# Relative-position products of both head groups in one 64-column matmul, columns before rows

## The chip, the cores and the metric

The kernel runs on one core of a Trainium2 chip. A core has TensorE (PE in the profile, with its weight loads listed apart as PEld), VectorE (DVE), ScalarE (ACT), GpSimd (POOL) and SyncE (SP), which here issues nearly all DMA transfers. Each engine works through its own list in order, and semaphores hold an instruction back until what it needs is there. The metric is the time of one execution on the device in microseconds (us), as the median of several runs. Lower is better.

## The reference

Eight images of 32x32 positions and 256 channels pass a first layer (group norm; a 3x3 convolution to 192 channels; beside it an attention of 8 heads with relative positions, 64 channels), then a second layer (layer norm, single-head attention over the 1024 positions), then a mixture of experts. What matters here is the relative part of the first attention. For every head and every query position, the logits get a term by the column distance and a term by the row distance:

```
rel = jnp.einsum('bnxyd,md->bnxym', q, rel_k)      # 63 distances m, 8 numbers d per head
rel = rel_to_abs(rel)                              # distance -> absolute column (or row) of the key
...
logits = jnp.einsum('bnid,bnjd->bnij', qf, kf)
logits = logits + rel_w + rel_h
weights = jax.nn.softmax(logits, axis=-1)
```

## The kernel before

**Stages.** For each image b the first part runs `first_layer(b)` and then `second_layer(b)`; after all eight images come the experts. The order on each engine is written out by hand. `fill.send(us)` puts pieces of the convolution (`pc`, line 481) or of the values (`pvv`, line 451) of an image between other work, by a fixed budget of microseconds and not by what is idle, so TensorE's list does not adapt to how long things take.

**Units.** The attention of the first layer is done in four `Unit`s per image: two halves of the queries by two groups g of four heads (HG = 4, NG = 2). A Unit's operand `F` is loaded by DMA when the Unit is made: lines 503 from the DRAM tile `fds` (keys' queries and the column features) and lines 507 from the DRAM tile `fys` (the row features). It is 2 x 768 KB and 4 x 128 KB. `score` (line 522) multiplies F with `KM` and DVE takes the maximum (line 529).

**The relative products.** `features(b, qs, qx)` makes what goes into `fds` and `fys`. It is a generator that is advanced eight times per image (a *piece* each). `qs` holds the queries of both groups row by row; `qx` is the same turned column by column, which GpSimd copies from `qs` (line 400). For each group and for each of rows (`which == 0`, table `bhs`, named `th` in the trace) and columns (`which == 1`, `bws`, `tw`), there are 32 matmuls, one for each row or column i, with a slice of the table as the stationary operand and 32 queries as the moving one (line 419). They fill one PSUM tile `prel` of 2 x 512 columns. A piece is 16 of these matmuls. After 32, the tile leaves PSUM in two halves: ACT copies each to `rel` rounded to fp32r (line 436), DVE writes the remainder beside it (line 437), and SP sends `rel` to `fys` (line 440) or `fds` (line 444).

**Where the pieces stand.** Pieces 1 and 2 of the next image stand at the end of `first_layer`. Pieces 3 to 8 stand in the first six of the eight steps of `second_layer`, called it0 to it5 here. A step (`Attention.scores`) is: the logits `lg` (line 754, four matmul passes of 512 columns), their maximum (757) and its scaling (758) on DVE, the exponential `pr` on ACT (760), then `beside()`, which advances the generator and sends some convolution, and then `turn()`, which transposes the exponentials of the step before (772) and copies them to `pt` (775 on DVE, 777 on ACT). Every second step, `finish` forms the product of a block of 256 queries with the values (`po`, line 832), ACT copies it to `os` (836), and TensorE multiplies it with the output weights (`pa`, 843). Unit 0 of the next image is made after piece 4, Unit 1 after piece 8; their first scores stand in the steps it6 and it7.

**Buffers that tie these together.** `lg_tile` hands out two PSUM tiles of two banks, in turn, to `lg`, `prel` and many others. A `prel` tile is held from its first piece until DVE has read it. `pt_tile` hands out three SBUF tiles for the `rel` tiles and for the `pt` of the blocks. Before, the `rel` of piece 6 takes the buffer that the first block's `pt` leaves, so its copy waits for that block's `po`.

At the start (image 0) there is nothing beside the pieces but convolution: `fill.send(1.5)` and `next(rel)` four times, then Unit 0, four times, then Unit 1.

Of the kernel before, what the change touches and what calls it, by code (L numbers as in the profile page):

```python
# [10 lines left out]
FP = mybir.dt.float32  # L11
FR = mybir.dt.float32r
I32 = mybir.dt.int32
AF = mybir.ActivationFunctionType
ALU = mybir.AluOpType
# [3 lines left out]
P = 128  # L19
B, HH, WW, C = 8, 32, 32, 256  # L20
S = HH * WW
# [3 lines left out]
HG = 4  # L25
NG = NH // HG
# [12 lines left out]
def kernel(  # L39
# [26 lines left out]
    nc = tc.nc  # L66
# [40 lines left out]
    with ExitStack() as ph:  # L107
        wp = ph.enter_context(tc.tile_pool(name="wp", bufs=1))
        work = ph.enter_context(tc.tile_pool(name="work", bufs=1))
# [16 lines left out]
        def lg_tile(name):  # L126
            return ps_lg.tile([P, 2, 512], FP, tag="lg", name=name)
# [7 lines left out]
        def pt_tile(name, dt=FP):  # L135
            return work.tile([P, 2048], dt, tag="pt", name=name, bufs=3)
# [69 lines left out]
        rel = []  # L206
        M = 2 * HH - 1
        for n, table in (("h", key_rel_h), ("w", key_rel_w)):
# [7 lines left out]
            tab = pt_tile(f"tab{n}")  # L216
# [11 lines left out]
            t = wp.tile([P, M * HG], FR, tag=f"t{n}", name=f"t{n}")  # L228
# [4 lines left out]
        bhs, bws = rel  # L233
# [177 lines left out]
        def features(b, qs, qx):  # L411


            for g in range(NG):
                for which in range(2):
                    pr = lg_tile("prel").rearrange("p a s -> p (a s)")
                    tab, src = ((bhs, qs), (bws, qx))[which]
                    for i in range(32):
                        nc.tensor.matmul(  # L419
                            pr[:, i * 32 : (i + 1) * 32],  # L420
                            lhsT=tab[:, (WW - 1 - i) * HG : (2 * WW - 1 - i) * HG],
                            rhs=src[:, g, i * 32 : (i + 1) * 32],
                            start=True,
                            stop=True,
                        )
                        if i == 15:
                            yield None
                    t = pt_tile("rel", FR).rearrange("p (l s) -> p l s", l=2)
                    for half in range(2):
                        c = slice(half * 512, (half + 1) * 512)  # L430
                        if which == 0:
                            ps, hi, lo = pr[:, c], t[:, 0, c], t[:, 1, c]
                        else:
                            ps = pr.rearrange("p (x y) -> p y x", y=HH)[:, half * 16 : half * 16 + 16, :]
                            hi, lo = (t[:, l, c].rearrange("p (y x) -> p y x", x=WW) for l in range(2))
                        nc.scalar.copy(hi, ps)  # L436
                        nc.vector.tensor_tensor(lo, ps, hi, ALU.subtract)  # L437
                    tb = t.bitcast(FP)
                    if which == 0:
                        nc.sync.dma_start(out=fys[b % 2][g].rearrange("l p s -> p l s"), in_=tb)  # L440
                    else:
                        dst = fds[b % 2][g][R_M * HG : (R_M + 64) * HG].rearrange("(l p) s -> p l s", p=P)
                        for p in (slice(HG, 64), slice(64, P)):
                            nc.sync.dma_start(out=dst[p], in_=tb[p])
                    yield None

        def values(b):
            pv = mi_tile("pvv").rearrange("p (j c) -> p j c", c=DK)
# [354 lines left out]
        def second_layer(b, sec, rel):  # L803
            more = b + 1 < B
            st2 = work.tile([P, NT, 6], FP, tag="lst2", name="lst2")
            units = []
            if more:
                fill.dense.insert(min(1, len(fill.dense)), values(b + 1))
            pieces = [2]

            def beside():
                if more and pieces[0] < 8:
                    next(rel)
                    pieces[0] += 1
                    if pieces[0] in (4, 8):
                        units.append(Unit(b + 1, pieces[0] // 4 - 1))
                    fill.send(0.6)
                else:
                    ahead(2)

            def ahead(n):
                for _ in range(n if units else 0):
                    units[0].score()
                fill.send(0.6)

            att.beside = beside
            for ib in range(S // IB):

                def finish(pt, rc, ib=ib):
                    po = ps_po.tile([P, 512], FP, tag="po", name="po1")  # L830
                    for jc in range(NT):
                        nc.tensor.matmul(  # L832
                            po[:, 0:IB], lhsT=sec.v[:, jc, :], rhs=pt[:, jc, :], start=jc == 0, stop=jc == NT - 1
                        )
                    os = work.tile([P, 512], FP, tag="os", name="os1")[:, 0:IB]
                    nc.scalar.copy(os, po[:, 0:IB])
                    if ib >= 2:
                        ahead(2)
                    else:
                        fill.send(0.8)  # L840
                    pa = st_tile("pa1").rearrange("p (i c) -> p i c", c=C)
                    for i in range(NIB):
                        nc.tensor.matmul(
                            pa[:, i, :], lhsT=os[:, i * P : (i + 1) * P], rhs=wo, start=True, stop=True
                        )
                    for i in range(NIB):
                        tt = T[b][:, ib * NIB + i, :]
                        nc.vector.scalar_tensor_tensor(tt, pa[:, i, :], rc[:, i : i + 1], tt, ALU.mult, ALU.add)
                        nc.vector.bn_stats(st2[:, ib * NIB + i, :], tt)

                blk = Block(finish)
                for i in range(NIB):
                    it = ib * NIB + i
                    att.scores(blk, i, sec.qk[:, 0, it * P : (it + 1) * P], sec.qk[:, 1], blk.rs, 1.0 / math.sqrt(U))
            ahead(2)
            att.drain(ahead)
            sums[b] = st2
            return units
# [36 lines left out]
        with tc.manual_schedule():  # L895
            nc.scalar.preload_act_table_set(LNEXP)
            fill.chains.append(normalise(0))
            while fill.chains:
                fill.send(1.0)
            rel = features(0, *queries(0))  # L900
            keys(0)
            fill.dense.insert(min(1, len(fill.dense)), values(0))
            units = []
            for g in range(NG):
                for i in range(4):
                    fill.send(1.5)
                    next(rel)
                units.append(Unit(0, g))
            fill.send(5.0)
            for b in range(B):  # L910
                sec, rel = first_layer(b, units)
                units = second_layer(b, sec, rel)
            fill.chains.append(token_mean(B - 1))
            fill.finish()
# [273 lines left out]
```

## Time and profile before

| | |
|---|---|
| median of 3 runs | 2906.44 us (2900.96 to 2912.57) |
| the profiled execution: time, and span from its first to its last instruction | 2906.21 us, 2904.4 us |
| busy share of the span: PE, PEld, DVE, ACT, POOL | 88%, 58%, 45%, 33%, 10% |
| matmuls of line 419, and mean granted TensorE clock | 1024; 0.96 of full speed |

Busy shares are sums over an engine's list; matmuls are pipelined and their ends modelled, so a busy PE is not a PE at its peak. Which work sets the end is read from the chain that ended last, and, at one place, from the timeline: each line there has the start, the duration, the engine, the source line, the operation, the tiles, and in square brackets the idle time before it and who ended that.

### The profile page before, as it was taken

The page shows a single profiled execution, that of the slowest core. Times are in us where ns is not written, and L with a number is a line of the kernel's source. Part 1 is how long each engine was busy: PE and PEld are TensorE (multiplying, and loading weights), DVE is VectorE, ACT ScalarE, POOL GpSimd, SP SyncE. Part 2 cuts the span into 40 slices and gives each one's busy share as a digit, 9 for nine tenths or more (in the row PEclk, how much of TensorE's full clock was granted, in tenths as well). Part 3 has the DMA queues.
Part 4 walks back from the last instruction along what each step waited for, and adds up shares of the span by engine and source line. Part 5 has one row for each costly group of instructions (what it writes and reads, how often), then busy time and mean ns, then how long its engine had stood idle before and what let it go on. Part 6 is the DMA issues. An engine that isn't in the chain of part 4 may idle for free.

```text
span 2904.4 us, 30948 instructions
## 1 busy us (share of the span) xinstructions
PE 2560.5 (88%) x12395; PEld 1685.4 (58%) x12395; DVE 1296.2 (45%) x2327; ACT 965.3 (33%) x1679; POOL 301.0 (10%) x196
## 2 busy tenths in 40 slices
PE   4899879997998799979987998799889769999998
PEld 3865665565656555655475556555654346666665
DVE  4454256426643564366335634662457252333232
ACT  0045214531452145214521552154225422223222
POOL 3011001100110011001100110011000021111110
PEclk7899889999999999999999999999999989999999
DMA  3621233133313321342144114312421031112110
GB/s 99 140 56 38 65 80 74 29 70 94 71 31 80 90 56 31 87 97 42 30 90 99 38 36 95 88 38 41 108 55 30 1 106 58 58 58 73 58 51 22
DMA packets 89761, 186.12 MB, mean 64 GB/s; under 512 B 8161, under 2 KB 36714, under 8 KB 87314
## 3 DMA queue, kind: packets, MB, share of 16 engines
q1 hardware_dynamic: 86962, 182.04, 26.6%
q8 instruction: 98, 1.61, 0.2%
q10 hardware_dynamic: 2656, 2.10, 0.2%
q14 instruction: 45, 0.37, 0.0%
HBM read 112.15 MB, written 62.52 MB: 60 GB/s over the span
## 4 chain that ended last, share of the span: by engine, by line
PE 76%; DVE 15%; ACT 5%; DMA 2%; issue 2%; SPq 1%; POOL 0%; ACTq 0%; DVEq 0%
PE pc L481 11%; PE po L573 9%; PE st L558 9%; PE py L1115 8%; PE phd L1097 8%; DVE mx L529 6%; PE lg L522 6%; PE prel L419 4%; PE po L832 4%; PE lg L754 3%; PE pq L653 2%; ACT PT L565 2%; PE tp L772 2%; PE pmean L874 1%; DMA T<-in_x_dram 1%
## 5 line engine op out<-in xcount | busy, mean ns | idle before, releaser
L565 ACT ACTIVATE PT<-st 128x512 f32<-128x512 f32 x1024 | 598.5, 598 | 492.5 <-PE st L558 452.9
L529 DVE TENSOR_REDUCE mx<-lg 128x1 f32<-128x1024 f32 x512 | 603.7, 1217 | 296.0 <-PE lg L522 295.9
L481 PE MATMUL pc<-convw,gpad 128*128 128x192 f32 x2304 | 506.0, 341 | 55.1 <-DVE T L489 33.6
L558 PE MATMUL st<-F,KM 128*128 128x512 f32 x1024 | 479.7, 474 | 19.6 <-ACT PT L565 11.6
L481 PEld LDWEIGHTS pc<-convw,gpad 128*128 128x128 f32 x2304 | 404.3, 196 | 109.5 <-DVE T L489 42.7
L522 PE MATMUL lg<-KM,F 128*128 128x512 f32 x1024 | 345.5, 424 | 73.9 <-ACT pr L760 32.9
L558 PEld LDWEIGHTS st<-F,KM 128*128 128x128 f32 x1024 | 192.2, 190 | 297.3 <-ACT PT L565 177.4
L573 PE MATMUL po<-PT,vk 128*32 128x512 f32 x2048 | 284.0, 617 | 0.0
L522 PEld LDWEIGHTS lg<-KM,F 128*128 128x128 f32 x1024 | 184.4, 190 | 143.0 <-DVE mx L529 50.3
L1115 PE MATMUL py<-w,hT 128*128 128x256 f32 x1024 | 237.3, 385 | 0.0
L1097 PE MATMUL phd<-n2T,w 128*128 128x512 f32 x512 | 222.9, 593 | 0.0
L1115 PEld LDWEIGHTS py<-w,hT 128*128 128x128 f32 x1024 | 189.9, 190 | 45.6 <-issue 22.4
L1122 DVE TENSOR_TENSOR r<-py,n 128x256 f32<-128x256 f32 x64 | 27.2, 425 | 308.4 <-PE py L1115 308.4
L1097 PEld LDWEIGHTS phd<-n2T,w 128*128 128x128 f32 x512 | 97.0, 191 | 115.5 <-issue 108.4
L352 POOL TENSOR_TENSOR T<-T,l0b 128x2048 f32<-128x2048 f32 x8 | 36.5, 4558 | 1145.2 <-PE tpx L311 1145.2
L591 DVE RECIPROCAL rc<-pa 128x16 f32<-128x16 f32 x32 | 8.3, 258 | 307.1 <-PE pa L588 307.1
L760 ACT ACTIVATE pr<-lg,nm 128x1024 f32<-128x1024 f32 x64 | 71.4, 1115 | 201.8 <-DVE nm L758 201.8
L754 PE MATMUL lg<-nqk 128*128 128x512 f32 x256 | 129.8, 633 | 0.0
L437 DVE TENSOR_TENSOR rel<-prel,rel 128x512 fp32r<-128x512 f32 x64 | 44.3, 692 | 190.6 <-ACT rel L436 190.6
L641 POOL TENSOR_TENSOR T<-T,n 128x256 f32<-128x256 f32 x64 | 48.3, 774 | 755.1 <-DVE n L638 755.1
L832 PE MATMUL po<-pt,v 128*128 128x256 f32 x512 | 121.1, 391 | 0.4 <-DVE pt L775 0.4
L1104 ACT ACTIVATE hT<-phd,b1c 128x512 f32<-128x512 f32 x128 | 86.3, 686 | 97.6 <-PE phd L1097 97.4
(223 smaller groups left out, 2441.4 us busy)
## 6 DMA issues: line engine op xcount, KB each, us to landing
F<-fd SPq DMA_DIRECT2D x64, 768.0 KB
fy<-rel SPq DMA_DIRECT2D x16, 1024.0 KB
F<-fy SPq DMA_DIRECT2D x128, 128.0 KB
w<-in_L_ffn_W_dram SPq DMA_DIRECT2D x32, 512.0 KB
T<-in_x_dram SPq DMA_DIRECT2D x8, 1024.0 KB
scr<-kqh SPq DMA_DIRECT2D x64, 128.0 KB
fd<-kqh SPq DMA_DIRECT2D x32, 256.0 KB
KM<-kd SPq DMA_DIRECT2D x32, 256.0 KB
```

Of the source, the lines that this page charges most:

```text
L419: nc.tensor.matmul(pr[:, i * 32 : (i + 1) * 32], lhsT=tab[:, (WW - 1 - i) * HG : (2 * WW - 1 - i) * HG], rhs=src[:, g, i * 32 : (i + 1) * 32],
L481: nc.tensor.matmul(pc[:, 0:CO], lhsT=gflat[:, dx, kc, t * P + dy * WW : (t + 1) * P + dy * WW], rhs=convw[:, (dy * 3 + dx) * KC + kc, :], ...
L522: nc.tensor.matmul(lg[:, a, :], lhsT=self.F[:, a, hl, i * P : (i + 1) * P], rhs=KM[:, self.g * HG + hl, a * 512 : (a + 1) * 512], start=Tr ...
L529: nc.vector.tensor_reduce(self.mx[:, i, hl : hl + 1], lg.rearrange("p a s -> p (a s)"), AX.X, ALU.max, negate=True)
L558: nc.tensor.matmul(st, lhsT=KM[:, self.g * HG + hl, j * P : (j + 1) * P], rhs=self.F[:, j // 4, hl, :], start=True, stop=True,)
L565: nc.scalar.activation(self.pts[j][:, hl, :], st, AF.Exp)
L573: nc.tensor.matmul(self.po[32 * hl : 32 * hl + 32, :], lhsT=vk[:, j, (self.g * HG + hl) * (DH + 1) : (self.g * HG + hl) * (DH + 1) + 32], ...
L754: nc.tensor.matmul(lg[:, h, :], lhsT=q, rhs=k[:, h * 512 : (h + 1) * 512], start=True, stop=True)
L832: nc.tensor.matmul(po[:, 0:IB], lhsT=sec.v[:, jc, :], rhs=pt[:, jc, :], start=jc == 0, stop=jc == NT - 1)
L1097: nc.tensor.matmul(phd, lhsT=ws[k][0][:, kc, f * P : (f + 1) * P], rhs=n2T[:, kc, q * 512 : (q + 1) * 512], start=kc == 0, stop=kc == KC - 1,)
L1104: nc.scalar.activation(hT[:, k * NF + f, :], phd, AF.Gelu, bias=b1c[:, f, k * B + b : k * B + b + 1])
L1115: nc.tensor.matmul(py, lhsT=hT[:, k * NF + f, j * P : (j + 1) * P], rhs=ws[k][1][:, f, :], start=False, stop=k == TOPK - 1 and f == NF - 1,)
```

## The change

`features` makes one matmul for both groups: the moving operand is `src[:, :, i*32:(i+1)*32]`, 2 x 32 columns, so there are 64 matmuls of 64 columns per image where there were 128 of 32. The order is now columns first (first half of the columns, second half), then rows (first half, second half). A PSUM tile holds 16 rows or columns of both groups, and the groups are parted when ACT and DVE read it, with 64 elements from one row or column to the next. A piece is 8 matmuls, and there are eight pieces as before, with as many copies, of the same size.

The column features of group 0 are collected over two tiles in the buffer of `kqh` (tag `kqh`), those of group 1 in a `pt` buffer, and go to `fds` after piece 4, for both groups. The row features go to `fys` in halves, after pieces 6 and 8, for both groups. Unit 0 is now made after piece 6, and Unit 1 after piece 8; at the start both are made after all eight pieces.

```diff
...
         def features(b, qs, qx):
 
 
-            for g in range(NG):
-                for which in range(2):
-                    pr = lg_tile("prel").rearrange("p a s -> p (a s)")
-                    tab, src = ((bhs, qs), (bws, qx))[which]
-                    for i in range(32):
-                        nc.tensor.matmul(
-                            pr[:, i * 32 : (i + 1) * 32],
-                            lhsT=tab[:, (WW - 1 - i) * HG : (2 * WW - 1 - i) * HG],
-                            rhs=src[:, g, i * 32 : (i + 1) * 32],
-                            start=True,
-                            stop=True,
+            turned = [
+                work.tile([P, 2, S], FR, tag="kqh", name="rel"),
+                pt_tile("rel", FR).rearrange("p (l s) -> p l s", l=2),
+            ]
+            for which, half in ((1, 0), (1, 1), (0, 0), (0, 1)):
+                pr = lg_tile("prel").rearrange("p a (i g s) -> p (a i) g s", g=NG, s=32)
+                tab, src = ((bhs, qs), (bws, qx))[which]
+                for n in range(16):
+                    i = half * 16 + n
+                    nc.tensor.matmul(
+                        pr[:, n],
+                        lhsT=tab[:, (WW - 1 - i) * HG : (2 * WW - 1 - i) * HG],
+                        rhs=src[:, :, i * 32 : (i + 1) * 32],
+                        start=True,
+                        stop=True,
+                    )
+                    if n == 7:
+                        yield None
+                if which == 0:
+                    rows = pt_tile("rel", FR).rearrange("p (g l s) -> p g l s", g=NG, l=2)
+                for g in range(NG):
+                    if which == 0:
+                        ps = pr[:, :, g, :]
+                        hi, lo = (rows[:, g, l].rearrange("p (y x) -> p y x", x=WW) for l in range(2))
+                    else:
+                        ps = pr[:, :, g, :].rearrange("p x y -> p y x")
+                        hi, lo = (
+                            turned[g][:, l].rearrange("p (y x) -> p y x", x=WW)[:, :, half * 16 : half * 16 + 16]
+                            for l in range(2)
                         )
-                        if i == 15:
-                            yield None
-                    t = pt_tile("rel", FR).rearrange("p (l s) -> p l s", l=2)
-                    for half in range(2):
-                        c = slice(half * 512, (half + 1) * 512)
-                        if which == 0:
-                            ps, hi, lo = pr[:, c], t[:, 0, c], t[:, 1, c]
-                        else:
-                            ps = pr.rearrange("p (x y) -> p y x", y=HH)[:, half * 16 : half * 16 + 16, :]
-                            hi, lo = (t[:, l, c].rearrange("p (y x) -> p y x", x=WW) for l in range(2))
-                        nc.scalar.copy(hi, ps)
-                        nc.vector.tensor_tensor(lo, ps, hi, ALU.subtract)
-                    tb = t.bitcast(FP)
+                    nc.scalar.copy(hi, ps)
+                    nc.vector.tensor_tensor(lo, ps, hi, ALU.subtract)
                     if which == 0:
-                        nc.sync.dma_start(out=fys[b % 2][g].rearrange("l p s -> p l s"), in_=tb)
-                    else:
+                        nc.sync.dma_start(
+                            out=fys[b % 2][g][:, :, half * 512 : half * 512 + 512].rearrange("l p s -> p l s"),
+                            in_=rows.bitcast(FP)[:, g],
+                        )
+                    elif half == 1:
+                        tb = turned[g].bitcast(FP)
                         dst = fds[b % 2][g][R_M * HG : (R_M + 64) * HG].rearrange("(l p) s -> p l s", p=P)
                         for p in (slice(HG, 64), slice(64, P)):
                             nc.sync.dma_start(out=dst[p], in_=tb[p])
-                    yield None
+                yield None
 
         def values(b):
             pv = mi_tile("pvv").rearrange("p (j c) -> p j c", c=DK)
...
                 if more and pieces[0] < 8:
                     next(rel)
                     pieces[0] += 1
-                    if pieces[0] in (4, 8):
-                        units.append(Unit(b + 1, pieces[0] // 4 - 1))
+                    if pieces[0] in (6, 8):
+                        units.append(Unit(b + 1, pieces[0] // 2 - 3))
                     fill.send(0.6)
                 else:
                     ahead(2)
...
             keys(0)
             fill.dense.insert(min(1, len(fill.dense)), values(0))
             units = []
+            for i in range(8):
+                fill.send(1.5)
+                next(rel)
             for g in range(NG):
-                for i in range(4):
-                    fill.send(1.5)
-                    next(rel)
                 units.append(Unit(0, g))
             fill.send(5.0)
             for b in range(B):
```

## The prediction

> **What bounds the kernel now.** I read the chain that ended last first: which engine's work stands on the path, and how much of it is the line that the change halves.
>
> ```profile
> PE 76%; DVE 15%; ACT 5%; DMA 2%; issue 2%; SPq 1%; POOL 0%; ACTq 0%; DVEq 0%
> PE pc L481 11%; PE po L573 9%; PE st L558 9%; PE py L1115 8%; PE phd L1097 8%; DVE mx L529 6%; PE lg L522 6%; PE prel L419 4%; PE po L832 4%; PE lg L754 3%; PE pq L653 2%; ACT PT L565 2%; PE tp L772 2%; PE pmean L874 1%; DMA T<-in_x_dram 1%
> ```
>
> The path is TensorE's, and the relative products (`prel L419`) hold 4% of it, about 120 us. The chain always passes through a busy engine, so 4% is a ceiling of what halving can give (60 us), not the gain. The instructions of that line come next:
>
> ```profile
> L419 PEld LDWEIGHTS prel<-scr,th x512: 186/192/337, 60.1 to 2071.5; 128*128 128x128 f32 x171
> L419 PE MATMUL prel<-scr,th x512: 254/263/580, 60.1 to 2071.5; 128*128 128x32 f32 x171
> ```
>
> Each of them has its own weight load of 128 columns for only 32 moving ones. What a piece of 16 costs, and who waits for whom around it, stands in the timeline of one second layer (image 6, which makes the features of image 7):
>
> ```profile
> 2054.88 1.86 PEld L419 LDWEIGHTS prel<-scr,tw 128*128 128x128 f32 x16 [1.82 <-issue]
> ...
> 2057.44 1.98 PE L754 MATMUL lg<-nqk 128*128 128x512 f32 x4
> ...
> 2060.99 1.11 ACT L760 ACTIVATE pr<-lg,nm 128x1024 f32<-128x1024 f32 x1 [3.60 <-DVE nm L758]
> ...
> 2062.25 1.98 PE L754 MATMUL lg<-nqk 128*128 128x512 f32 x4
> ...
> 2073.26 3.62 PE L832 MATMUL po<-pt,v 128*128 128x256 f32 x16
> ...
> 2076.97 0.59 ACT L436 CAST rel<-prel 128x512 fp32r<-128x512 f32 x1 [4.09 <-PE po L832]
> ...
> 2079.27 0.39 ACT L836 COPY os<-po 128x256 f32<-128x256 f32 x1
> ...
> 2079.71 1.13 PE L843 MATMUL pa<-wo,os 128*128 128x256 f32 x4 [2.19 <-ACT os L836]
> ...
> 2090.26 0.58 ACT L436 CAST rel<-prel 128x512 fp32r<-128x512 f32 x1
> ...
> 2094.60 0.38 ACT L836 COPY os<-po 128x256 f32<-128x256 f32 x1
> ...
> 2095.03 1.13 PE L843 MATMUL pa<-wo,os 128*128 128x256 f32 x4 [0.17 <-ACT os L836]
> ```
>
> Two things are to be seen. First, the `lg` of it2 starts at 2062.25, just after the exponential of it1 (2060.99 + 1.11, and a readout of 0.19 behind it: 2062.2): it takes the PSUM tile which that exponential frees. TensorE happened to have just enough work to arrive there in time. Second, at it3 the `rel` copy on ACT waited 4.09 us for `po`, and `os`, queued behind it, cost TensorE 2.19 us before `pa`; at it5 the copy had no wait.
>
> **Part 1: the products.** 16 loads take 1.92 us in the piece at 2050.06, so one follows another by (1.92 - 0.19)/15 = 0.115 us, and a piece of 8 saves 8 x 0.115 = 0.92 us. That holds if the load still sets the pace with 64 columns. No fp32r matmul of 64 is in the trace. Ends: 0.115 (32 columns) and 0.161 (line 481, 192 columns, 32 loads in 5.17 us), which makes the saving 0.92 or 0.55. I take 0.92, because line 663 with 128 columns does 16 loads in 1.86 us, 0.111 each. Not below nothing: there is no load more than before.
>
> How much of the eight savings reaches the end, step by step in this image:
> - Piece 1 (end of the first layer): TensorE runs without a gap into it and `pa` behind it feeds DVE. On the path: 0.92.
> - Piece 2: the copies of its tile, the `lg` of it0 and piece 3 all follow its end. On the path: 0.92.
> - Pieces 3, 4 and 5: the next `lg` then waits for the exponential (at 2057.4, 2062.2 and 2068.0), whose own chain of `lg` 2.0, maximum 1.2, scaling 0.2 and exponential 1.3 has no `prel` in it. Saved time becomes idle time of TensorE: 0.
> - Piece 6: from the `lg` of it3 on, TensorE works without a gap to the end of `po` at 2076.88. On the path: 0.92.
> - Piece 7: again the exponential (over by 2085.3, `lg` at 2085.6): 0.25.
> - Piece 8: without a gap to the end of the second `po` at 2094.03: 0.92.
>
> **Part 2: the buffers.** In the built program's order of waits the piece-6 copy no longer waits for the first `po`; the copy of transposed exponentials (lines 775 and 777) does instead. So `os` stands behind one ACT copy and not behind two copies with a DVE subtraction between: 0.1 + 0.59 + 0.38 = 1.1 us after `po` where it was 2079.66 - 2076.88 = 2.8. Gain 1.65. But the piece-8 copy now takes the buffer that the second `po` leaves, which the one before did not. Behind it on ACT stand the second copy, the `pt` copy and `os`; on DVE two subtractions and, in this image, the copy that frees the convolution's PSUM tile, for which 8 `pvv` matmuls on TensorE wait. After that `po`: copy 0.59, subtraction 0.69, copy 0.59, subtraction 0.69 with gaps 2.7; tile copy 0.35; `pvv` 1.0: `pa` at about 4.1, where it was 2095.03 - 94.03 = 1.0. Loss 3.1.
>
> Sum for this image: 4 x 0.92 + 0.25 + 1.65 - 3.1 = 2.5 us. Images 1 to 5 come to the same within 0.2. In image 0 piece 4 ran at half clock (16 matmuls in 4.21 us) and was late itself, and no `pvv` waits in it5: about 5. Over seven images 6 x 2.5 + 5 = 20 us. Ends for an image: nothing regained in it3 and the slow pace, 2.5 - 1.65 - 1.5 = -0.6; every piece on the path and no loss in it5, 8 x 0.92 + 1.65 = 9.
>
> Free of cost: the PSUM reads with stride 64 (the copies of `th` and `tw`, straight and turned, are all between 575 and 587 ns, the subtractions between 690 and 693); two more issues on SP per image (0.39 each; SP stands idle for 13 us before the next); Unit 0's load after piece 6. That load is hidden by it4 and it5: issued about 2075, behind 1 MB of row features (3.5 us), and 12.6 us long (Unit 1's from 2098.87 to 2111.5), it lands near 2091, and its first score comes near 2096. Without this 5 us cover each us later costs seven.
>
> **Part 3: the start.** Here there is no such cover:
>
> ```profile
> 60.15 3.56 PE L419 MATMUL prel<-scr,th 128*128 128x32 f32 x16 [6.64 <-DMA scr<-kqh]
> 62.55 1.93 POOL L400 CAST scr<-scr 128x1024 fp32r<-128x1024 f32 x1 [0.45 <-DMA scr<-kqh]
> 92.96 1.26 SPq L503 DMA_DIRECT2D F<-fd  x2
> 109.70 1.22 PE L522 MATMUL lg<-KM,F 128*128 128x512 f32 x4
> ```
>
> Columns first need both turned copies, so piece 1 starts at 64.5 and not 60.1: 4.4 later. The eight pieces take 24.4 us (cold clock) and save 12.2, so the last ends near 96 instead of 103.4. But Unit 0's load, issued at 92.96 before, now stands behind all row features, near 99.2. With 12.6 us of its own and the last 1 MB ahead of it, it lands near 114, and the first score, at 109.7 before, waits: +4.5. Ends: 7.8 gained if the load comes in time, 9 lost if the idle time also keeps the clock low.
>
> Sum against the profiled execution (2906.2, and so 0.2 from the median): 2906.2 - 20 + 4.5 = **2890 us**.
>
> **The clock, a rule that speaks against it.** The change turns matmul time into short idle gaps. Windows of 10 us in image 0 and image 6 (busy time by engine, then the granted clock, DMA share and GB/s):
>
> ```profile
> 342.00:352.00 10.00, 10.00 (x35) 7.68 (x33) 3.36 (x5) 2.96 (x5) 0.00 (x0) 0.52 0.17 41
> 2093.00:2103.00 10.00, 7.50 (x39) 5.43 (x38) 6.64 (x12) 2.35 (x5) 0.00 (x0) 1.00 0.66 170
> ```
>
> A window with a quarter of TensorE idle kept clock 1.00; the slow one was full and began before. The slow clock made image 0's stretch from the first `lg` to the first `pa` 33.1 us (333.8 to 366.9), where image 6 took 27.8: 5.3 us an occurrence. I take no further occurrence.
>
> The Trainium skill's page "TensorE: Matmul & The Clock Gate", section "A second HAM failure mode: psum-queue depth-cycling", says that micro-idling between groups of matmuls while PSUM buffers cycle is enough to make the clock oscillate. By it each second layer would be throttled, and the estimate would end above the time before; the 1.00 above disagrees.
>
> **The rivals.**
> - *All on the path* (0.10): the exponential's chain also moves forward. 56 x 0.92 = 52 saved, less 4.5 at the start: 2859. For it: 4% in the chain; against: the exponentials' ends above.
> - *Nothing left* (0.20): it3's 1.65 isn't regained. 6 x 0.85 + 3.3 - 4.5 = 4 us: 2902.
> - *The clock falls* (0.15), the slower side: seven second layers at 5.3 us, 37 - 16 = +21: 2927. Three occurrences cancel the gain; six make a loss over 0.5%. For it: image 0's windows; against: image 6's.
> - That the products are not halved is ruled out by the built order: 64 per image.
>
> **How the numbers follow.** The forecast has 0.55, with its own range 2876 to 2902. 0.5% is 14.5 us, about what a measurement of this kernel can tell from no change; the bound at 2892 lies inside that range. Faster: 0.10 and 0.40 of the forecast; same: 0.15 of it, 0.20, and 0.02 of the clock case; slower: 0.13. The range takes in the full gain's near side and half of the clock case: 2862 to 2912.
>
> **What would show it.** Right: 512 instructions on line 423 with loads 0.115 apart; gaps of about 0.9 us before the `lg` of it1, it2 and it3, ended by the exponential; about 0.5 us instead of 2.19 before `pa` in it3; ACT's piece-8 copy waiting for `po`; the first score near 114; images 283.6 us apart, where the runs of 32 `pc` loads from 313.3 to 2031.9 stood 1718.6/6 = 286.4 apart. Wrong: loads more than 0.13 apart, clock under 0.9 in the second layers, or a wait for F in it6.

## The result and the profile after

The changed kernel takes 2914.40 us (median of 19 runs, 2908.09 to 2917.72). The kernel before took 2905.18 us beside it (19 runs, 2897.66 to 2917.18). The ratio is 1.0032, with an interval from 1.0021 to 1.0042: a third of a per cent slower, where 2890 (2862 to 2912) was predicted. The profiled execution took 2916.05 us, with a span of 2914.3 and a mean granted clock of 0.949; before, the span was 2904.4 and the clock 0.960.

The chain that ended last, by engine and by line:

```profile
PE 73%; DVE 17%; ACT 6%; issue 2%; DMA 1%; SPq 1%; POOL 0%; ACTq 0%; DVEq 0%; POOLq 0%
PE pc L492 11%; PE po L584 9%; PE st L569 9%; PE py L1126 8%; PE phd L1108 8%; DVE mx L540 6%; PE lg L533 6%; PE po L843 4%; PE lg L765 3%; PE pq L664 2%; ACT PT L576 2%; DVE nm L768 2%; ACT pr L771 2%; PE pmean L885 2%; PE py L1123 1%
```

The relative products (4% before) have left the list. DVE and ACT took their place: the maximum `nm` and the exponential `pr` of the second layer, 2% each. The products themselves, by form (min, median and max duration in ns):

```profile
L423 PEld LDWEIGHTS prel<-scr,tw x256: 186/192/337, 63.8 to 2064.6; 128*128 128x128 f32 x128
L423 PE MATMUL prel<-scr,tw x256: 267/277/1042, 63.8 to 2064.7; 128*128 128x64 f32 x128
L423 PEld LDWEIGHTS prel<-scr,th x256: 186/192/338, 85.2 to 2090.0; 128*128 128x128 f32 x128
L423 PE MATMUL prel<-scr,th x256: 268/277/595, 85.2 to 2090.0; 128*128 128x64 f32 x128
```

There are 512, and they are as cheap as hoped. A matmul of 64 columns has a median of 277 ns where one of 32 had 263, and a burst of 8 loads takes 0.97 us, so one follows another by (0.97 - 0.19)/7 = 0.111 us. The timeline of the second layer of image 6, from it1 on:

```profile
2062.13 1.98 PE L765 MATMUL lg<-nqk 128*128 128x512 f32 x4 [0.74 <-ACT pr L771]
...
2067.20 1.98 PE L765 MATMUL lg<-nqk 128*128 128x512 f32 x4 [0.99 <-ACT pr L771]
...
2072.98 1.98 PE L765 MATMUL lg<-nqk 128*128 128x512 f32 x4 [0.54 <-ACT pr L771]
...
2081.84 1.13 PE L854 MATMUL pa<-wo,os 128*128 128x256 f32 x4 [0.35 <-ACT os L847]
...
2091.40 3.62 PE L843 MATMUL po<-pt,v 128*128 128x256 f32 x16
2095.11 0.59 ACT L444 CAST rel<-prel 128x512 fp32r<-128x512 f32 x1 [2.87 <-PE po L843]
...
2098.09 1.25 PE L462 MATMUL pvv<-qkvw,gpad 128*128 128x64 f32 x8 [3.06 <-DVE T L500]
...
2099.12 2.02 PE L854 MATMUL pa<-wo,os 128*128 128x256 f32 x4
...
2100.94 2.58 PE L765 MATMUL lg<-nqk 128*128 128x512 f32 x4
```

Up to it5 this is the timeline that the prediction drew. The `lg` of it1, it2 and it3 wait for the exponential, and `pa` of it3 waits 0.35 us instead of 2.19. At it5 ACT's copy waits for the second `po`, TensorE stands idle for 3.06 us, and `pa` starts 2099.12 - (2091.40 + 3.62) = 4.10 us behind that `po`. What the prediction did not draw is the last two lines. `pa` takes 2.02 us, not 1.13, and the next `lg` 2.58, not 1.88. Nothing waits inside them; the clock fell.

Windows of that stretch (busy us and instructions of PE, PEld, DVE, ACT and POOL; then the granted clock, DMA share and GB/s):

```profile
2092.09:2095.50 3.41, 2.93 (x14) 2.24 (x12) 0.00 (x0) 0.54 (x3) 0.00 (x0) 1.00 0.29 31
2095.50:2098.91 3.41, 0.82 (x7) 0.83 (x8) 2.32 (x5) 1.55 (x4) 0.00 (x0) 1.00 0.47 174
2098.91:2102.33 3.42, 3.42 (x9) 2.35 (x9) 1.11 (x3) 0.00 (x0) 0.00 (x0) 0.50 1.02 280
2102.33:2105.74 3.41, 1.66 (x5) 0.57 (x3) 2.77 (x5) 0.68 (x1) 0.00 (x0) 1.00 0.97 242
```

In the second of them TensorE was busy for 0.82 us of 3.41. The third is at half clock from its first moment to its last. The windows are cut at the instants at which the clock changes, and these instants repeat: read in steps of 0.1 us over the whole trace, each stretch at half clock lasts 3.41, 6.83, 10.24 us and so on, and every beginning lies on one grid of 3.4133 us, within 0.01 us from 150 us to the end. The stretch between two neighbouring points of this grid is called a window below, and a half-clock window when its clock is 0.50. The Trainium skill's page "TensorE: Matmul & The Clock Gate", section "What's actually happening", names such a free-running window of 3413 ns, and the traces agree with that. It lets the clock fall after an idle window, and there the traces ask for less: here 0.82 us of work in the window did not keep it.

At the start the chain shows what was forecast:

```profile
101.30 0.62 SPq L514
...
102.80 10.01 DMA F<-fy
112.81 2.48 issue
115.29 0.76 PE lg L533
```

Unit 0's load is issued at 101.30 (92.96 before), and the first score starts at 115.29 instead of 109.70: 5.6 us later, where 4.5 were put down.

### The profile page after: what moved, and what is told of

The parts are those of the page before. It is cut to its first block, busy times and chain, and to the rows that moved or that the text cites. A ratio compares the mean times of both kernels' runs of the same rounds, so it can differ in the third digit from the quotient of the medians.

```text
span 2914.3 us, 29997 instructions
## 1 busy us (share of the span) xinstructions
PE 2535.9 (87%) x11883; PEld 1644.4 (56%) x11883; DVE 1300.4 (45%) x2327; ACT 963.5 (33%) x1679; POOL 300.9 (10%) x196
## 4 chain that ended last, share of the span: by engine, by line
PE 73%; DVE 17%; ACT 6%; issue 2%; DMA 1%; SPq 1%; POOL 0%; ACTq 0%; DVEq 0%; POOLq 0%
PE pc L492 11%; PE po L584 9%; PE st L569 9%; PE py L1126 8%; PE phd L1108 8%; DVE mx L540 6%; PE lg L533 6%; PE po L843 4%; PE lg L765 3%; PE pq L664 2%; ACT PT L576 2%; DVE nm L768 2%; ACT pr L771 2%; PE pmean L885 2%; PE py L1123 1%
## 5 line engine op out<-in xcount | busy, mean ns | idle before, releaser
L569 PE MATMUL st<-F,KM 128*128 128x512 f32 x1024 | 479.4, 474 | 19.6 <-ACT PT L576 11.6
L765 PE MATMUL lg<-nqk 128*128 128x512 f32 x256 | 141.8, 683 | 17.0 <-ACT pr L771 17.0
L768 DVE TENSOR_REDUCE nm<-lg 128x1 f32<-128x1024 f32 x64 | 78.2, 1222 | 93.7 <-PE lg L765 93.7
```

The lines of the kernel that those rows point to most:

```text
L569: nc.tensor.matmul(st, lhsT=KM[:, self.g * HG + hl, j * P : (j + 1) * P], rhs=self.F[:, j // 4, hl, :], start=True, stop=True,)
L765: nc.tensor.matmul(lg[:, h, :], lhsT=q, rhs=k[:, h * 512 : (h + 1) * 512], start=True, stop=True)
L768: nc.vector.tensor_reduce(nm, lg, AX.X, ALU.max, negate=True)
```

## The experiments

Three theories stood at first. **A:** the wait at it5 costs its 3.1 us, and the gap that it makes brings the clock down besides. **B:** the clock falls because shorter products leave more small gaps, whatever that wait does. **C:** the loss comes from Unit 0's later load and its traffic.

### The wait taken away from the changed kernel

The last tile of row features gets a buffer that is free by then (line 433):

```diff
-                    rows = pt_tile("rel", FR).rearrange("p (g l s) -> p g l s", g=NG, l=2)
+                    if half == 0:
+                        rows = pt_tile("rel", FR).rearrange("p (g l s) -> p g l s", g=NG, l=2)
+                    else:
+                        rows = work.tile([P, 2, S], FR, tag="kqh", name="rel").rearrange("p g (l s) -> p g l s", l=2)
```

> Changed kernel, with the last piece's tile of row features (images 1 to 7) in the buffer of the query projections, which is free by then, instead of the buffer that the second `po` leaves. Nothing else is changed. Theory A (the copies that wait for `po` in it5 cost 3.1 us themselves, and the gap of TensorE over 3 us that they make lowers the granted clock behind it, 3 to 4 us more): 7 x 6.1 to 7.1 = 43 to 50 us less than the changed kernel's 2914, so 2864 to 2871; in image 6 `pa` of it5 takes 1.13 us and starts 1 us after `po`; the granted clock from `po` to the end of the second layer is 1.00. Theory B (the clock falls because products are shorter and there are more small gaps, whatever the wait): 7 x 3.1 = 22 less, 2893, with clock 0.5 to 0.8 still there behind it5. Theory C (the loss is the later load of Unit 0 and its traffic): 2908 to 2916, no change.

Measured: 2878.43 us, ratio to the kernel before 0.9899 (0.9879 to 0.9919). The timeline of it5 in image 6:

```profile
2066.78 3.62 PE L846 MATMUL po<-pt,v 128*128 128x256 f32 x16
2067.53 0.58 ACT L447 CAST rel<-prel 128x512 fp32r<-128x512 f32 x1
...
2070.49 1.10 PE L465 MATMUL pvv<-qkvw,gpad 128*128 128x64 f32 x8
...
2071.43 1.10 PE L857 MATMUL pa<-wo,os 128*128 128x256 f32 x4
```

The copy runs beside `po`, TensorE has no gap, and `pa` takes 1.10 us. The clock is 1.00 from it5 to it6 in all seven images, where it was 0.78 to 0.88 in the changed kernel. That is theory A, 36 us of it, and theory C is out. The place is the one that was named: from the exponential of it5 to that of it6 the seven images together take 68.6 us instead of 102.6, and these 34.0 us are the whole difference of the two spans (33.8). But less than the 43 to 50 came, because the clock behind the gap costs less than the 3 to 4 us an image put down for it (the next experiment has its price). Half-clock windows remain elsewhere: behind it6 in images 0, 3 and 4, and in it0 of four images.

### The wait put into the kernel before

The same copies, waits and products as before, but the tile of piece 2 is taken out of the ring, which moves the wait for the second `po` to piece 8:

```diff
-                    t = pt_tile("rel", FR).rearrange("p (l s) -> p l s", l=2)
+                    if g == 0 and which == 0:
+                        t = work.tile([P, 2, S], FR, tag="kqh", name="rel")
+                    else:
+                        t = pt_tile("rel", FR).rearrange("p (l s) -> p l s", l=2)
```

> Kernel before, with its 512 products of line 419 twice over (32 columns, 1024 in all) and its order unchanged; only the tile of piece 2 (first row features) lies in the buffer of the query projections. By the order of waits this shifts the ring: the piece-6 copies no longer wait for the first `po` (a gain of 1.65 us an image in it3) and the piece-8 copies wait for the second `po` (a loss of 3.1 in it5), the same two waits as in the changed kernel. Theory A: 7 x (3.1 - 1.65) = 10 for the waits and 7 x 3 to 4 for the clock behind the gap: 2906 + 31 to 38 = 2937 to 2944, with granted clock 0.5 to 0.8 behind it5 although no product is shorter. Theory B (the clock needs the shorter products): 2916 and clock 1.00 there.

Measured: 2923.23 us, ratio 1.0061 (1.0041 to 1.0082). It5 of image 6 in the timeline, then two windows behind it:

```profile
2106.18 0.59 ACT L439 CAST rel<-prel 128x512 fp32r<-128x512 f32 x1 [3.76 <-PE po L835]
...
2109.15 1.68 PE L454 MATMUL pvv<-qkvw,gpad 128*128 128x64 f32 x8 [3.06 <-DVE T L492]
2110.62 2.02 PE L846 MATMUL pa<-wo,os 128*128 128x256 f32 x4
```

```profile
2106.07:2109.49 3.42, 0.36 (x4) 0.34 (x4) 2.05 (x4) 1.94 (x4) 0.00 (x0) 1.00 0.00 0
2109.49:2112.90 3.41, 3.41 (x12) 2.92 (x12) 0.49 (x3) 0.00 (x0) 0.00 (x0) 0.50 0.90 245
```

The gap of 3.06 us and the half clock behind it are there with products of 32 columns, in images 1 to 6. In image 0 the copies of piece 8 do not wait in this kernel, the step from it5 to it6 takes 10.59 us (10.60 before), and the clock there is 1.00. So theory B cannot explain the half clock behind it5: the clock did not stay at 1.00, and the time lies above its 2916. The size fell short of the 31 to 38 us expected, because I had taken seven waits where there are six, and 3 to 4 us of clock an image, where one half-clock window costs about half its length: from the exponential of it6 to that of it7 it is 6.55 us at full clock and 8.2 with one such window, 1.65 more.

### The gap filled, the wait left in

Five matmuls of 256 columns, read by nobody, behind the second `po` of the changed kernel:

```diff
+                    if more and ib == 1:
+                        for n in range(5):
+                            nc.tensor.matmul(
+                                po[:, IB : 2 * IB], lhsT=sec.v[:, n, :], rhs=sec.nT[:, 0, 0:IB], start=True, stop=True
+                            )
                     os = work.tile([P, 512], FP, tag="os", name="os1")[:, 0:IB]
```

> Changed kernel, with 5 more matmuls of 256 columns on TensorE right behind the second `po` of each second layer with features (0.45 us each, 2.3 together, into the unused half of the `po` bank; their result is read by nobody). The wait of the copies stays as it is; only the gap of TensorE is filled. Theory A: the wait of it5 still costs its 3.1 us, but the gap before `pa` shrinks from 3.1 to 0.8 us, the clock stays 1.00 behind it, and the 3 to 4 us an image that the clock cost come back: 2914 - 21 to 28 = 2886 to 2893. If the clock has another cause: 2914 to 2918, with 0.5 to 0.8 behind it5 as before.

Measured: 2903.82 us, ratio 0.9990 (0.9976 to 1.0004): 10 us faster than the changed kernel with more work in it, and half of what was expected. In the profile the clock from it5 to it6 is 1.00 in all images, and this step takes 87.1 us in the seven images together instead of 102.6. But from it6 to it7 one window or two are still at half clock in five images of seven. The gaps there are not the wait's: they are two of 2.34 us, in which TensorE waits for the exponentials of it6 and it7, and the kernel before had them as well (2.33 and 2.35).

### The wait of it3 alone

Only the tile of piece 6 is taken out of the ring of the kernel before (the edit of the second experiment with `g == 1`).

> Kernel before, with only the tile of piece 6 in the buffer of the query projections: its copies no longer wait for the first `po`, and no other copy takes the wait over. This is the 1.65 us of it3 alone, without the products of 64 columns. If it reaches the end: 2906 - 7 x 1.65 = 2894.5. If another wait takes its place: 2903 to 2908. `pa` in it3 starts 0.5 us behind `os` rather than 2.19 late.

Measured: 2898.27 us, ratio 0.9983 (0.9969 to 0.9996): 6 us, about half. The time from it3 to it4 did fall by 1.83 us in every image. It was given back behind it6, where all seven images now have a window at half clock and in the kernel before only image 0 had one. The gap in front of it is the same. Windows of the kernel before on its own grid, then of this kernel on its own:

```profile
2095.87:2099.28 3.41, 2.48 (x8) 1.06 (x6) 2.97 (x7) 0.00 (x0) 0.00 (x0) 1.00 0.56 157
2099.28:2102.70 3.42, 2.02 (x15) 1.93 (x16) 2.44 (x4) 1.21 (x2) 0.00 (x0) 1.00 0.68 176
2102.70:2106.11 3.41, 2.17 (x6) 0.77 (x5) 2.21 (x4) 0.73 (x2) 0.00 (x0) 1.00 1.05 229
```

```profile
2087.63:2091.04 3.41, 1.07 (x4) 0.49 (x3) 2.84 (x4) 1.20 (x2) 0.00 (x0) 1.00 0.21 57
2091.04:2094.45 3.41, 3.41 (x15) 3.12 (x14) 1.92 (x2) 0.28 (x1) 0.00 (x0) 0.50 1.05 281
```

Before, the grid cut the gap in two and left 2.48 and 2.02 us of work on the two sides. Here the whole gap lies in one window, 1.07 us of work are left in it, and the next window is at half clock. So this gap of 2.33 us costs 1.65 or nothing, by where it falls on the grid. Counted over the fourteen traces from 300 to 2300 us, 339 of the 344 full-clock windows in which TensorE was busy for less than 0.45 of the window were followed by half clock; with more than about half, nearly all went on at full clock. There are exceptions, above all in it0, where windows with 0.64 to 0.72 of work were followed by half clock. What the clock's monitor takes for work there is open.

### The gaps of it6 and it7 filled

Four matmuls of 256 columns between the two scores of it6, and four in it7 (`att.po` is the last `po` tile, kept for this):

```diff
                 else:
-                    ahead(2)
+                    if more:
+                        units[0].score()
+                        for n in range(4):
+                            nc.tensor.matmul(
+                                att.po[:, IB : 2 * IB], lhsT=sec.v[:, n, :], rhs=sec.nT[:, 0, 0:IB], start=True, stop=True
+                            )
+                    ahead(1 if more else 2)
```

First in the kernel with its own tile, then in the kernel before.

> The kernel with its own tile for the last row features, and 4 matmuls of 256 columns more (1.8 us, read by nobody) in each of the two gaps of 2.34 us in which TensorE waits for the exponential of it6 and of it7, in the seven second layers with features. In the traces so far the granted clock changes only on a grid of 3.413 us, and a window of the grid is at 0.50 when TensorE was busy for less than about 0.45 of the window before. Theory (clock grid): with the gaps filled no window of it6 or it7 is slow whatever the phase; 3 such in seven images of the profiled run go, at 1.65 us each, and more in runs with a worse phase: 2866 to 2874, although work is added. Rival (the gaps aren't the cause): 2878 to 2890, since 14 x 0.3 to 0.6 us of added work reach the path.

> Kernel before with the same 4 added matmuls in the gaps of it6 and it7 and nothing else. Its gaps there are as long (2.33 and 2.35 us), but its profiled run had the slow window behind them only in image 0. Theory (clock grid, the phase differs from run to run): the median falls by 2 to 8 us (2896 to 2902) and the highest runs come down, because the phases that are unlucky there no longer cost up to 7 x 1.65. Rival: 2904 to 2910, no gain or a loss.

Measured: 2872.74 us, ratio 0.9890 (0.9873 to 0.9907), and 2898.84, ratio 0.9988 (0.9976 to 1.0000). In both profiles the clock from it6 to it7 is 1.00 in all seven images, and that step takes 6.55 us in each: adding up to 3.6 us of work to a second layer lengthened nothing there. The highest run of the kernel before came down from 2914.11 to 2907.10. As expected, then, but by medians these gains (5.7 and 3.6 us) are hardly larger than their intervals.

### The early load, and the products of 32 columns

Two more edits of the kernel with its own tile, each alone. Unit 0's load is issued after piece 6 at the start as well:

```diff
             for i in range(8):
                 fill.send(1.5)
                 next(rel)
-            for g in range(NG):
-                units.append(Unit(0, g))
+                if i in (5, 7):
+                    units.append(Unit(0, (i - 5) // 2))
```

And the product of 64 columns is split again into one for each group:

```diff
-                        pr[:, n],
+                            pr[:, n, g],
...
-                        rhs=src[:, :, i * 32 : (i + 1) * 32],
+                            rhs=src[:, g, i * 32 : (i + 1) * 32],
```

> The kernel with its own tile for the last row features, and at the start (image 0 alone) Unit 0's load is issued after piece 6 instead of after piece 8, as the second layer already does it. Theory: at the start the load of Unit 0 stands behind the second half of the row features; in front of them it lands 5 us sooner, the first score comes near 110 instead of 115, and the whole moves by 4 to 5: 2878 - 4.5 = 2874. Rival: the first score then waits for the last piece or for the keys, and nothing or 2 us are gained: 2876 to 2880.

> The kernel with its own tile for the last row features, but with products of 32 columns again: two matmuls for each row or column, one for each group of heads, 1024 in all; order, copies, buffers and loads stay. This takes the 64 columns away and leaves everything else. Theory of the prediction's sum (0.92 us for a piece that is on the path: 3.9 us an image, and 12 at the start where all eight pieces are in the way): 2878 + 7 x 3.9 + 10 to 12 = 2915 to 2918. Rival (the gain is that of the order and the buffers, and the halved products only turn into idle time): 2878 + 12 for the start at most, 2880 to 2890.

Early load: 2874.93 us, ratio 0.9901 (0.9884 to 0.9918). The first score starts at 109.03 us; it was 115.29 in the changed kernel and 117.60 in the profile of the kernel with its own tile. So the step at the start was read rightly; whether the 3.5 us by medians are real, these intervals don't say. Split products: 2918.28, ratio 1.0053 (1.0038 to 1.0069), on the value expected for the prediction's terms. With the wait out of the way the 64 columns are worth 40 us by medians. They were not all lost in idle time: from image to image the kernel with split products takes 3.70 us longer (284.69 against 280.99, by the first exponentials of images 0 and 6), where 3.9 were put down. Part of the agreement is luck, though. At the start the first score comes 5.7 us later (123.33 against 117.60) and not 10 to 12, and the two profiled executions, the fastest run of the one and the slowest of the other, differ by 29.7.

### The prediction's sum with the clock held

The changed kernel, wait included, with both fillings (5, 4 and 4 matmuls).

> The changed kernel with its wait for the second `po` left in place, and TensorE kept busy in three gaps of each second layer with features: 5 added matmuls of 256 columns behind the second `po` and 4 in each of the gaps of it6 and it7 (13 a layer, 5.9 us of work that nobody reads). If the sum of the prediction was right in all but the clock, this is its number: 2906 - 20 + 5.5 at the start = 2892, so 2886 to 2896, with 1.00 from it5 to the end of the second layer in every image. Rival (terms of the sum were wrong as well, and the clock is only a part of it): 2900 to 2912.

Measured: 2888.74 us, ratio 0.9960 (0.9944 to 0.9976). The prediction said 2890; against the kernel before beside it (2901.21) this is 12.5 less, where the sum with the measured start says 14.5, and the two profiles have nearly as many half-clock windows (52 and 51 after 300 us). The clock is 1.00 from it5 to it7 in every image, and at it5 the wait is still there. The timeline of image 6, with the five added matmuls in its second line (the trace has each of these matmuls as two instructions):

```profile
2071.23 3.62 PE L850 MATMUL po<-pt,v 128*128 128x256 f32 x16
2074.68 2.32 PE L855 MATMUL po<-nqk,v 128*128 128x256 f32 x10
2077.91 1.10 PE L462 MATMUL pvv<-qkvw,gpad 128*128 128x64 f32 x8 [0.90 <-DVE T L500]
2078.85 1.08 PE L866 MATMUL pa<-wo,os 128*128 128x256 f32 x4
```

`pa` starts 4.0 us behind `po`, as before the filling, but takes 1.08 us. This kernel also parts the loss at it5 into its two causes. From the exponential of it5 to that of it6 the seven images together take 102.6 us in the changed kernel, 87.1 here and 68.6 with the tile's own buffer. So the clock costs 15.5 us there, and the wait itself 18.5, where 7 x 3.1 = 21.7 were put down.

### Together

Own tile, early load and the filled gaps of it6 and it7; then the same with four more matmuls behind the last `pvv`, ahead of the `pc` that waits 2.34 us for `vk`; last, the kernel before with the freed piece-6 tile and the same fillings. What is new in it stands at the end of `values`:

```diff
+            for n in range(4 if b > 0 else 0):
+                nc.tensor.matmul(
+                    att.po[:, IB : 2 * IB], lhsT=qkvw[:, 0, 0:P], rhs=gflat[:, 1, 0, 0:IB], start=True, stop=True
+                )
             yield 0.23
```

> Own tile for the last row features, Unit 0's load after piece 6 at the start, and the 4 added matmuls in the gaps of it6 and it7: the three edits that were each tried with the own tile, together. If they add up: 2878.4 - 3.5 - 5.7 = 2869. If the load at the start and the clock there are one cause counted twice: 2872 to 2875.

> As the kernel with own tile, early load and filled it6 and it7, and 4 more added matmuls of 256 columns behind the last `pvv` of images 1 to 7, ahead of the `pc` that waits 2.34 us for `vk`: the slow windows behind that gap (one in the image read) go, at 1.65 each: up to 10 less, 2860 to 2868. Rival: `pa` and the scores queued behind the added work are on the path, 1.8 us an image: 2870 to 2882.

> Kernel before (products of 32 columns, its own order and start) with the three things that helped the changed kernel and are no part of the change: the piece-6 tile in the buffer of the query projections (the wait for the first `po` goes), and the added matmuls in the gaps of it6 and it7 and ahead of the `pc` that waits for `vk`. If the terms found so far add up: 2904 - 7 x 1.65 for the wait - 4 for the filled gaps of it6 and it7 - 6 for that of `vk` = 2882; and the products of 64 columns with their order are then worth 2882 - 2858 = 24 us. Rival (the filled gaps and the freed buffer give all the gain, the change itself nothing): 2860 to 2868.

Measured: 2866.11 us, ratio 0.9892 (0.9875 to 0.9909), so the three edits add up; 2857.88, ratio 0.9862 (0.9843 to 0.9882); and 2872.31, ratio 0.9904 (0.9884 to 0.9925). The second of them is the fastest kernel of the study, 43 us under the kernel before beside it. The last was expected at 2882 and came 10 us lower, 4 above the range in which the change itself would be worth nothing: in its profile the fillings took 11 half-clock windows away, not the 6 that I had counted on. Between the last two lies what the change with its repairs is worth when the clock is helped on both sides: 14 us by medians, not the 24 expected. The two ratios' intervals just fail to overlap. (The spans, 2853.2 and 2875.8, differ by 23, but they are those of the fastest run of the one and the slowest of the other.)

### The account

Each trace gives its half-clock windows after 300 us. With the terms of the prediction and 1.65 us for each such window more than before, the spans come out (all less the span before, 2904.4; terms: the wait of it5 3.1 and that of it3 1.65, seven times each, but that of it5 six times in the kernel before with both waits moved; 20 from the prediction's sum; 5.5 at the start, which the early load takes away):

| Kernel | Terms, us | Half-clock windows (before 51) | Sum, us | Span less that before, us |
|---|---|---|---|---|
| changed kernel | -20 + 5.5 | 66 | +10.3 | +9.9 |
| before, with both waits moved | +7.1 | 58 | +18.6 | +17.1 |
| before, wait of it3 gone | -11.6 | 53 | -8.3 | -8.2 |
| changed, gap of it5 filled | -14.5 | 58 | -3.0 | -3.7 |
| changed, all three gaps filled | -14.5 | 52 | -12.9 | -16.1 |
| own tile | -14.5 - 21.7 | 57 | -26.3 | -23.9 |
| own tile, it6 and it7 filled | -36.2 | 53 | -32.9 | -32.0 |
| before, it6 and it7 filled | 0 | 42 | -14.9 | -12.8 |
| own tile, early load, all filled | -41.7 | 43 | -54.9 | -51.2 |
| before, wait of it3 gone, filled | -11.6 | 40 | -29.8 | -28.6 |

None is off by more than 5 us, and neither are the three kernels left out of the table: early load -35.1 against -32.6, early load with filled it6 and it7 -38.4 against -40.7, and split products, with 27.3 us for the images and 11 for the start added back, +2.1 against +5.8. The windows were counted in one execution of each kernel, so the column is a reading of these traces and not a forecast for another run. Nor does every half-clock window cost 1.65: over the 60 runs of the kernel before that were taken beside the experiments, a line through their spans and the windows that follow from their granted clocks rises by only 0.9 us a window (an estimate, with a correlation of 0.71).

## Why the prediction was wrong

The other terms held. The pace of the loads (0.115 put down, 0.111 measured), the pieces that reach the end and those that only make idle time, the 1.65 us at it3 (`pa` waits 0.35 instead of 2.19, against about 0.5), the 3.1 us at it5 in image 6 (`pa` 4.10 behind `po`, against 4.1) and the start (115.29 against "near 114") are all in the trace. At the start the eight pieces ended at 98.1 instead of near 96, so the load was issued at 101.30 instead of 99.2, and the first score came 5.6 us later and not 4.5. The kernel with the clock held, 12.5 us under the kernel before where these terms give 14.5, bears out their sum; the median of the split products, 2918.28, does so too, but with the luck told above. (The sum itself is 2890.7, put down as 2890.)

**The step that failed** is the one on the clock, "I take no further occurrence". The changed kernel has 15 half-clock windows more than the kernel before, 15 x 1.65 = 25 us, which ate the 20 us of gain and left +5.5 from the start. Ten of them lie between the exponentials of it5 and it6, where the kernel before had none; they are the 15.5 us measured above. Six more lie between those of it6 and it7, seven against one, and this step takes 57.1 us in the seven images together instead of 47.5; the gap there was not new, only its place on the grid. The images were to be 283.6 us apart and are (2060.87 - 343.23)/6 = 286.3, from the first exponential of image 0 to that of image 6; before, they were 286.4 by the same measure.

Two faults lie in that step. First, its evidence was too coarse: a 10 us window with a quarter of TensorE idle kept clock 1.00, but the clock is decided over 3.41 us, and a mean over three such windows can't show whether one of them was nearly empty. Second, the sum itself had made the gap. I had put down 3.1 us of TensorE waiting for the `pvv` and `pa` of it5 as a loss of 3.1 and never asked what so long a gap does to the clock, though the longest gap in the second layer of image 6 before was 2.35.

The section of the Trainium skill that was weighed there ("TensorE: Matmul & The Clock Gate", "A second HAM failure mode: psum-queue depth-cycling") pointed the right way, a clock that goes up and down, and this case's first reading of the trace against it was wrong. But the short waits between groups of matmuls did not do it here: behind those of 0.54 to 0.99 us in it1 to it3 of image 6 the clock stayed at 1.00. The price in the rival that was set beside it, 5.3 us for every second layer, was too high; the measured price is 1.65 us for a half-clock window of it6, and 15 of them.

Of the rivals, *the clock falls* (0.15, 2927) had a falling clock, at 13 us too much. But it blamed the saved time that turns into idle gaps. The kernel with its own tile has all of these gaps and full clock behind it5, and the kernel before with the moved wait has none of them and half clock there: the one long gap did most of it, ten windows of the 15. Whether shorter products have a small part in the rest isn't shown. The kernel with its own tile has six half-clock windows more than the kernel before (57 and 51), the same kernel with split products has 51, and each is one execution with its own place on the grid. *Nothing left* (0.20, 2902) is ruled out by it3, whose wait is gone (9.70 us from it3 to it4 in image 6 instead of 12.43), and *all on the path* (0.10, 2859) by the gaps ahead of `lg` in it1 to it3.

The median, 2914.40 us, lies above the range of 2862 to 2912.

## What to carry to other kernels

When a sum contains a new gap of the tensor engine as long as the 3.06 us here, put down the gap and also the matmuls behind it at half clock, and read the granted clock in windows as short as the steps in which it changes. When a change moves a tile through a ring of buffers, write down which reader each later tile now waits for: one buffer that was free anyway was worth 36 us here, more than the change itself was meant to bring. An engine that waits can be given work that nobody reads, if it ends before the wait does: it cost nothing in these runs and bought back up to 1.65 us for each window.

## What the hardware showed that I had not expected

- The granted clock changes only on a grid of 3.4133 us, between 1.00 and 0.50, and a window's clock follows from the work in the one before it: up to 1.40 us of work in 3.41 brought half clock in it6, and 1.48 and more kept full clock, with one exception at 1.66 in the fourteen traces.
- The phase of that grid against the first instruction differs from run to run (0.08 us in the profiled run of the kernel before, 2.08 in that of its copy without the wait of it3, each taken modulo 3.4133). The same gap of 2.33 us therefore cost 1.65 us in seven images of one kernel and nothing in six of the other. In both, the exponential of it6 follows that of the image before by 283.5 to 286.5 us from image 2 on, which is 83.1 or 83.9 windows and so close to a whole number: these images share their luck. In the kernel with its own tile the distance is 81.8 to 82.6 windows, and some of its images were hit and others not.
- More work made the kernel faster: the fastest one issues 12 matmuls that nobody reads for each of seven images.
